# Chains of small numbers on GpSimd, other PSUM tiles and a later sum in a four-layer graph network

## The chip, the cores and the metric

The kernel runs on one core of a Trainium2 chip. The metric is the device time of one execution in microseconds (us). The engines are called as in the profile: PE (TensorE's matmuls), PEld (its weight loads), DVE (VectorE), ACT (ScalarE), POOL (GpSimd), SP (SyncE, which here only issues DMAs).

## What is computed

Four graph layers follow one another on x (4096 nodes x 64 numbers), all with the same dense 0/1 adjacency matrix `adj` (4096 x 4096, 64 MB), each as `x = layernorm(x + layer(x, adj))`:

```python
# layer 0: mean over the neighbours, a linear map, relu, unit length
h = (adj @ x + x) / (adj.sum(1, keepdims=True) + 1)
z = relu(concat([x, h], 1) @ W + b);  y = z / norm(z)
# layers 1 and 3: attention in hyperbolic space
adj_att = sigmoid(left[:, None] + right[None, :] + b_att) * adj
support = einsum('ij,ijd->id', adj_att, logmap(x[:, None], x[None]))
y = proj(expmap(x, support))
# layer 2: the last 100 neighbours, weight halved with each further one
rank = cumsum(adj != 0, axis=1)
y = w(rank) @ (x @ weight) + bias
```

`left` and `right` are one number per node, and `logmap` for a pair of nodes comes down to a function of a bilinear form of the two, so that a 128 x 1024 tile of pairs is a matmul and a few elementwise operations.

## The kernel before

Rows are cut into four groups of 1024 (`GROUPS`, 3 down to 0), columns into 32 blocks of 128 (`BLOCKS`, 31 down to 0). `load` (L655, on SP's queue) brings two blocks of one group, 1 MB, into one of six buffers. Every layer reads the whole matrix once.

**Attention, `attend`.** For one group, a loop over 16 pairs of blocks. For each block of a pair (k = 1, then 0): six matmuls into a tile `z` of 128 x 1024 (two banks of PSUM) from the edges (L945), `hi_lo` (L948) and `src` (L951); on ACT the sigmoid `sig` (L953) and the square `sq` of z (L956); on DVE `max(z, 0) * sig` into half of `t` (L959). For the pair: `(sq + HIGH**2) * t` on 128 x 2048 (L961, DVE). Then four f32 matmuls (eight records, L965) add `xe` times `t` to the group's sums `acc`. PSUM has two `z` tiles (four banks), two `acc` tiles, and two `aux` tiles for everything done by rows: eight banks.

**Row work.** Everything per node stands in generators: `move` (takes the group's sums through `expmap`, `proj`, the residual and the layernorm), `prepare` (the tables of the next attention), `linear` (a 64 x 64 map), `spread_left`, `end_0`, `end_2`. Numbers per node of a group are tiles of 128 x 8, so that nearly all of `move`, L1015 to L1079, is a chain of DVE operations on 8 elements per partition, with three calls of `rsqrt` (L673 to L679, ten operations each) and one tanh on ACT (L1034). Around it stand copies of the rows from `aux` (L1002, ACT), one product on GpSimd (L1007), two reductions on DVE (L1011, L1013), and at the end a product on GpSimd (L1081), one on DVE (L1082) and a sum on DVE (L1085). Row tiles have one buffer each.

**What sets the order.** `later` puts a generator in one of two queues. `tick(n)` counts places, and at each it resumes the generators whose time has come; the number that a generator yields (`soon`, `near`, `after`) is how many places it waits. In attention there are `rate` ticks behind each of a pair's two L959 and behind its L961. `need(tag)` ticks until a part is done. `held` and `free` keep row work from asking for an `aux` tile while another is in use. What is traced in this way is put in order by the framework's planner: in the attention layers it may place row work ahead of pair work on an engine where it thinks it ready; in layers 0 and 2 the order of PE and ACT is that of the program.

**Layer 2.** `count` makes the running count of neighbours: it adds to a tile `z`, by two matmuls for each 512 rows (L1386), what the block before and this one bring. ACT turns it into weights (Exp, L1395), and `add_up` adds weights times `halves` to the sums (four matmuls of 64 columns, L1401). `wide_pass` runs two groups side by side, `narrow_pass` one, twice. In the wide pass PE gets the count of one group, then the sums of the other, one behind.

The loop of the pairs before:

```python
zp = ps.tile([P, WW], F32, name="z")
...
V.scalar_tensor_tensor(t[:, k], zp, 0.0, sig, ALU.max, ALU.mult)
tick(rate)
...
V.scalar_tensor_tensor(t, sq, HIGH**2, t, ALU.add, ALU.mult)
for k in (1, 0):
    j = 2 * g + k
    for h in range(2):
        nc.tensor.matmul(acc[h * D : (h + 1) * D, :], xe[:, j, :], ...)
tick(rate)
```

Of the kernel before, what the change touches and what calls it, by code (L numbers as in the profile page):

```python
# [10 lines left out]
F32 = mybir.dt.float32  # L11
# [10 lines left out]
D = 64  # L22
# [36 lines left out]
def gnn_stack_kernel(  # L59
# [509 lines left out]
    def stream(fits):  # L569

        with ExitStack() as st:
# [9 lines left out]
            aux = pool("f_aux", 2, space=PSUM)  # L581
# [7 lines left out]
            FIXED = {mybir.EngineType.PE, mybir.EngineType.Activation}  # L589
            queues, place, done, held = ([], []), [0, 0], set(), []  # L590

            def tick(n):
                for _ in range(n):
                    place[1] += 1
                    for queue in queues:
                        while queue and queue[0][1] <= place[1]:
# [5 lines left out]
                            if wait:  # L602
                                break

# [24 lines left out]
            def near():  # L629

                return 3 if place[0] == 0 else 1

# [36 lines left out]
            def rsqrt(a, name):  # L669
# [10 lines left out]
                return r  # L680

# [73 lines left out]
            def curved(c, name, least):  # L755


                c2, sc, rsc, of_y, root, short = (
                    num(keep, name + n, 1)
                    for n in ("_c2", "_sc", "_rsc", "_of_y", "_root", "_short")  # L760
# [3 lines left out]
                V.tensor_mul(root, rsc, c)  # L764
                V.tensor_scalar(of_y, rsc, -((2.0 * UNIT) ** -0.5), None, ALU.mult)
# [3 lines left out]
                return c, c2, sc, rsc, of_y, root, short  # L769
# [21 lines left out]
            def prepare(layer, s, att, b_att, curve, least, good, small):  # L791


                c, c2, sc, rsc, of_y, root, short = curve
# [110 lines left out]

            def spread_left(s):
# [17 lines left out]
            def attend(layer, s, rate, then):  # L924
# [3 lines left out]
                acc = ps.tile([P, W], F32, name="acc")  # L928
                for g in reversed(range(NB // 2)):
# [4 lines left out]
                    sq = sb.tile([P, 2, WW], F32, name="sq")  # L934
                    t = sb.tile([P, 2, WW], F32, name="t")
                    for k in (1, 0):
# [3 lines left out]
                        zp = ps.tile([P, WW], F32, name="z")  # L940
                        for h in range(2):
# [9 lines left out]
                            nc.tensor.matmul(half, src[:, of], dst[:, to], start=False, stop=True)  # L951
                        sig = sb.tile([P, WW], F32, name="sig")
# [9 lines left out]
                    for k in (1, 0):  # L962
                        j = 2 * g + k
                        for h in range(2):
                            nc.tensor.matmul(  # L965
                                acc[h * D : (h + 1) * D, :], xe[:, j, :],
                                t[:, k, h * W : (h + 1) * W],
                                start=j == BLOCKS[0], stop=j == BLOCKS[-1],
                            )
                    tick(rate)  # L970
                sums = row.tile([P, W], F32, name="sums", bufs=2)
# [10 lines left out]
            def move(layer, s, sums, curve):  # L982
# [3 lines left out]
                c, c2, sc, rsc, of_y, root, short = curve  # L986
# [22 lines left out]
                yield near()  # L1009
                yield soon()  # L1010
# [4 lines left out]
                V.scalar_tensor_tensor(k, d, c2, sum_1, ALU.mult, ALU.add)  # L1015
                V.tensor_mul(k, k, rb[:, at])

                kx, t2, xt = nums("kx"), nums("t2"), nums("xt")
                V.tensor_mul(kx, k, x2g)
                V.scalar_tensor_tensor(t2, d, -2.0, kx, ALU.mult, ALU.add)  # L1020
                V.tensor_mul(t2, t2, k)
                V.tensor_add(t2, t2, uu)
                V.tensor_scalar(t2, t2, 1e-30, None, ALU.max)
                V.tensor_sub(xt, d, kx)
                yield soon()
# [3 lines left out]
                V.scalar_tensor_tensor(un, t2, root, rsqrt(t2, "r_t2"), ALU.mult, ALU.mult)  # L1029
                V.tensor_scalar(un, un, fac, short, ALU.mult, ALU.max)  # L1030
                th = nums("th")
                V.reciprocal(r_un, un)
# [50 lines left out]
                yield soon()  # L1083
                yield soon()
                V.tensor_add(x_of(layer + 1)[:, at, :], u, w)  # L1085
                yield after(72)

            def linear(layer, s, weights, finish):

# [420 lines left out]
```

## Time and profile before

| | |
|---|---|
| median of 3 runs | 1141.41 us (1140.45 to 1144.33) |
| the profiled execution's own time | 1140.81 us |
| its span, first to last instruction | 1139.1 us |
| PE, DVE, ACT, POOL busy in the span | 1021.6, 956.0, 821.2, 66.1 us |
| layer 0, up to the first L959 | 0 to 191 us |
| layer 1, to its last L961 | 191 to 532 us |
| layer 2, to layer 3's first L959 | 527 to 777 us |
| layer 3, to its last L961 | 777 to 1110 us |
| last `move` and store | 1110 to 1139 us |

A line of the profile's groups or of its timeline has the source line in the kernel, the engine, the operation, `out<-in` by the program's names, and sizes as partitions x elements. In a timeline the first two numbers are the start and the duration in us; the brackets at the end give idle time of the engine before the instruction and what ended it. Records of neighbouring instructions on an engine can overlap a little, so what an instruction takes from its engine is read from start to start. PE's durations are modelled, so there too the spacing is read.

### The profile page before, as it was taken

The page shows a single profiled execution, that of the slowest core. Times are in us where ns is not written, and L with a number is a line of the kernel's source. Part 1 is how long each engine was busy: PE and PEld are TensorE (multiplying, and loading weights), DVE is VectorE, ACT ScalarE, POOL GpSimd, SP SyncE. Part 2 cuts the span into 40 slices and gives each one's busy share as a digit, 9 for nine tenths or more (in the row PEclk, how much of TensorE's full clock was granted, in tenths as well). Part 3 has the DMA queues.
Part 4 walks back from the last instruction along what each step waited for, and adds up shares of the span by engine and source line. Part 5 has one row for each costly group of instructions (what it writes and reads, how often), then busy time and mean ns, then how long its engine had stood idle before and what let it go on. Part 6 is the DMA issues. An engine that isn't in the chain of part 4 may idle for free.

```text
span 1139.1 us, 13626 instructions
## 1 busy us (share of the span) xinstructions
PE 1021.6 (90%) x4949; PEld 391.2 (34%) x4949; DVE 956.0 (84%) x1882; ACT 821.2 (72%) x894; POOL 66.1 (6%) x97
## 2 busy tenths in 40 slices
PE   6999897899999899998999997798899999998981
PEld 3545544233333333332333232232333333333320
DVE  6687898999999899999653476528999999999996
ACT  0003216899989789787766778888898998987970
POOL 0020120000000000100100020000000001001001
PEclk8999998999999999999999999899999999999995
DMA  8999998545666466564988976676455665665500
GB/s 342 422 391 405 373 415 337 196 166 203 215 206 219 154 209 221 180 204 154 322 305 301 341 263 233 233 257 231 164 206 188 218 222 194 222 221 183 196 0 23
DMA packets 38419, 271.58 MB, mean 238 GB/s; under 512 B 4550, under 2 KB 4550, under 8 KB 5574
## 3 DMA queue, kind: packets, MB, share of 16 engines
q1 hardware_dynamic: 37440, 269.50, 65.8%
q10 hardware_dynamic: 902, 1.12, 0.3%
q8 instruction: 41, 0.67, 0.2%
q14 instruction: 36, 0.29, 0.1%
HBM read 269.55 MB, written 1.05 MB: 238 GB/s over the span
## 4 chain that ended last, share of the span: by engine, by line
DVE 53%; PE 29%; ACT 8%; DMA 6%; POOL 2%; issue 2%; ACTq 0%; SPq 0%; POOLq 0%; DVEq 0%
DVE t L959 21%; DVE t L961 20%; PE z L1386 10%; DMA edges<-in_adj_dram 6%; PE acc L1401 5%; PE acc L1243 4%; PE acc L965 2%; ACT sig L953 2%; ACT sq L956 2%; ACT sq L1395 1%; PE aux L1106 1%; PE aux L852 1%; PE z L945 1%; DVE junk L751 1%; PE z L951 1%
## 5 line engine op out<-in xcount | busy, mean ns | idle before, releaser
L953 ACT ACTIVATE sig<-left_b,right 128x1024 f32<-128x1024 f32 x256 | 293.8, 1149 | 46.5 <-DVE t L959 36.5
L959 DVE SCALAR_TENSOR_TENSOR t<-z,sig 128x1024 f32<-128x1024 f32 x256 | 310.0, 1216 | 5.9 <-ACT sq L956 5.0
L956 ACT ACTIVATE sq<-z,turn 128x1024 f32<-128x1024 f32 x256 | 281.5, 1106 | 22.8 <-PE z L951 20.7
L961 DVE SCALAR_TENSOR_TENSOR t<-sq,t 128x2048 f32<-128x2048 f32 x128 | 292.9, 2288 | 0.7
L965 PE MATMUL acc<-t,xe 128*64 128x512 f32 x1024 | 255.2, 611 | 28.5 <-DVE t L961 24.4
L945 PE MATMUL z<-edges,two_i 128*128 128x512 bf16 x512 | 201.7, 394 | 21.5 <-DVE t L959 21.5
L951 PE MATMUL z<-dst,src 74*128 74x512 f16 x512 | 195.2, 381 | 0.0
L948 PE MATMUL z<-lo_hi,hi_lo 128*128 128x512 f16 x512 | 194.1, 379 | 0.0
L1395 ACT ACTIVATE sq<-z,at_edge 128x512 bf16<-128x512 f32 (+1 forms) x192 | 153.0, 830 | 53.3 <-PE z L1386 51.9
L965 PEld LDWEIGHTS acc<-t,xe 128*64 128x64 f32 x1024 | 63.6, 137 | 163.0 <-DVE t L961 85.9
L751 DVE SCALAR_TENSOR_TENSOR t<-edges 128x2048 bf16<-128x2048 f32 x32 | 74.0, 2312 | 44.2 <-DMA edges<-in_adj_dram 44.1
L1386 PE MATMUL z<-edges,pass_by 128*128 128x512 bf16 x248 | 89.6, 401 | 15.9 <-ACT sq L1395 15.8
L945 PEld LDWEIGHTS <-two_i 128*128 128x128 bf16 x512 | 50.2, 98 | 143.8 <-issue 96.6
L1243 PE MATMUL acc<-edges,first 128*128 128x512 bf16 x256 | 80.6, 396 | 20.0 <-DMA edges<-in_adj_dram 19.8
L1386 PE MATMUL z<-edges,enter 128*128 128x512 bf16 x256 | 90.8, 397 | 0.0
L1401 PE MATMUL acc<-sq,halves 128*64 128x512 bf16 x512 | 82.6, 401 | 3.6 <-ACT sq L1395 2.9
L1243 PE MATMUL acc<-edges,third 128*65 128x512 bf16 x256 | 80.5, 396 | 0.0
L751 DVE SCALAR_TENSOR_TENSOR junk<-edges 128x2048 bf16<-128x2048 f32 x32 | 73.1, 2285 | 4.7 <-DMA edges<-in_adj_dram 4.5
L948 PEld LDWEIGHTS <-hi_lo 128*128 128x128 f16 x512 | 50.3, 98 | 68.8 <-issue 25.5
L951 PEld LDWEIGHTS <-src 74*128 74x128 f16 x512 | 49.2, 96 | 67.5 <-issue 2.3
L1081 POOL TENSOR_TENSOR w_att<-x,p 128x512 f32<-128x512 f32 x8 | 12.9, 1615 | 495.0 <-DVE q L1079 495.0
L1243 PEld LDWEIGHTS <-first 128*128 128x128 bf16 x256 | 24.1, 98 | 48.9 <-issue 21.3
(262 smaller groups left out, 771.3 us busy)
## 6 DMA issues: line engine op xcount, KB each, us to landing
edges<-in_adj_dram SPq DMA_DIRECT2D x256, 1024.0 KB, 4.9
x<-in_x_dram SPq DMA_DIRECT2D x4, 256.0 KB
out_dram<-x ACTq DMA_DIRECT2D x4, 256.0 KB
w_sb<-in_L_gnn_W_dram ACTq DMA_DIRECT2D x1, 32.0 KB, 5.1
given<-in_L_gnn_b_dram ACTq DMA_DIRECT2D x1, 0.2 KB
given<-in_L_gnn_bias_dram ACTq DMA_DIRECT2D x1, 0.2 KB
given<-in_L_gnn_b_att_dram ACTq DMA_DIRECT2D x1, 0.0 KB
given<-in_L_gnn_att_b_dram ACTq DMA_DIRECT2D x1, 0.0 KB
```

The source lines that it names most:

```text
L751: V.scalar_tensor_tensor(junk, a, 0.0, a, ALU.not_equal, ALU.not_equal, accum_out=odd[:, n : n + 1])
L945: nc.tensor.matmul(half, two_i, edge[:, at : at + W], start=True, stop=False)
L948: nc.tensor.matmul(half, hi_lo[:, of], lo_hi[:, to], start=False, stop=False)
L951: nc.tensor.matmul(half, src[:, of], dst[:, to], start=False, stop=True)
L953: nc.scalar.activation(sig, left_b, AF.Sigmoid, bias=right[:, j : j + 1])
L956: nc.scalar.activation(sq[:, k], zp, AF.Square, bias=turn, scale=-1.0 / UNIT)
L959: V.scalar_tensor_tensor(t[:, k], zp, 0.0, sig, ALU.max, ALU.mult)
L961: V.scalar_tensor_tensor(t, sq, HIGH**2, t, ALU.add, ALU.mult)
L965: nc.tensor.matmul(acc[h * D : (h + 1) * D, :], xe[:, j, :], t[:, k, h * W : (h + 1) * W], start=j == BLOCKS[0], stop=j == BLOCKS[-1],)
L1243: nc.tensor.matmul(accs[h][:m], lhs[:, j, :], edge[:, at : at + W], start=j == BLOCKS[0], stop=j == BLOCKS[-1],)
L1386: nc.tensor.matmul(z[:, h : h + W], lhs, rhs[:, h : h + W], start=j == BLOCKS[0], stop=True, skip_group_check=True,)
L1395: nc.scalar.activation(w, z[:, :n], AF.Exp, bias=at_edge, scale=-LN2)
```

## The change

- **GpSimd.** In `move`, for every group but a layer's last, the small operations and the last two large ones (L1082, L1085) go from DVE to GpSimd (`class Small`). There a `scalar_tensor_tensor` is two operations. The first step of each `rsqrt` (integers), the reciprocal of `den` and the two reductions stay on DVE. The reciprocal of `un` is replaced by a product and a minimum. The generator's waits become `pool_done(...)`.
- **Order.** `mark` makes every row instruction on PE, ACT or DVE that a tick traces follow, on its engine, the last pair instruction traced before it; from the second group of an attention layer on.
- **PSUM.** Three `z` tiles (six banks), one `acc`, one `aux`. In `end_0` the two halves take the one `aux` tile in turn. Layer 2's wide pass keeps the sums of both groups in the third `z` tile.
- **Sums later.** In `attend` a pair's four matmuls into `acc` come two pairs later, behind the first block's z matmuls of that pair (`in_order`). `sig` has three buffers.
- **Layer 2.** In the wide pass PE gets the counts of both groups, then the sums of both for the block before.
- **`linear` and the stores** behind a group go to the second queue, 9 ticks on, for every group but the last.

```diff
-            aux = pool("f_aux", 2, space=PSUM)
+            aux = pool("f_aux", 1, space=PSUM)
...
+            ROW_ENGINES = FIXED | {mybir.EngineType.DVE}
...
+            def mark(rows):
+                traced = nc.cur_bb.bb.instructions
+                for i in traced[seen[0] :]:
+                    if i.engine not in ROW_ENGINES:
+                        continue
+                    if not rows:
+                        pairs_last[i.engine] = i
+                    elif anchored[0] and i.engine in pairs_last:
+                        tc.add_manual_dep(
+                            i, pairs_last[i.engine].name,
...
+                seen[0] = len(traced)
 
             def tick(n):
                 for _ in range(n):
                     place[1] += 1
+                    mark(False)
...
+                    mark(True)
...
+            def pool_done(small, large=0):
+
+                return 2 + int(small * 0.2 + large * 0.9)
...
+            class Small:
...
+                def stt(self, out, in0, scalar, in1, op0, op1):
+                    if not self.on_pool:
+                        V.scalar_tensor_tensor(out, in0, scalar, in1, op0, op1)
+                        return
+                    t = nums("pool_t")
+                    nc.gpsimd.tensor_scalar(t, in0, scalar, None, op0)
+                    nc.gpsimd.tensor_tensor(out, t, in1, op1)
...
+                def rsqrt(self, a, name, small):
+
+                    r, t = nums(name), nums("rs_t")
+                    if self.on_pool:
+                        yield self.wait(small)
+                    V.tensor_scalar(
+                        r.bitcast(I32), a.bitcast(I32), -0.5, float(0x5F3759DF),
+                        ALU.mult, ALU.add,
+                    )
+                    for _ in range(3):
+                        self.mul(t, r, r)
+                        if self.on_pool:
+                            self.mul(t, t, a)
+                            self.ts(t, t, -0.5, 1.5, ALU.mult, ALU.add)
+                            self.mul(r, t, r)
...
@@ attend
+                def add_up(g, t, behind=None):
+
+                    for k in (1, 0):
+                        j = 2 * g + k
+                        for h in range(2):
+                            it = nc.tensor.matmul(
...
+                            if behind is not None:
+                                in_order(it.ins, behind.ins)
...
-                        zp = ps.tile([P, WW], F32, name="z")
+                        zp = z_tile()
...
+                        if k == 1:
+                            if len(lag) == 2:
+                                add_up(*lag.pop(0), last)
+                            sq = sb.tile([P, 2, WW], F32, name="sq")
+                            t = sb.tile([P, 2, WW], F32, name="t")
+                        sig = sb.tile([P, WW], F32, name="sig", bufs=3)
...
+                    lag.append((g, t))
                     tick(rate)
+                for args in lag:
+                    add_up(*args)
@@ move
+                G = Small(s != GROUPS[-1])
+                yield G.wait(0, 1) if G.on_pool else near()
                 V.tensor_reduce(uu, sq, AX.X, ALU.add)
                 yield soon()
                 V.tensor_reduce(d, w, AX.X, ALU.add)
                 yield soon()
+                yield soon()
+                G.stt(k, d, c2, sum_1, ALU.mult, ALU.add)
+                G.mul(k, k, rb[:, at])
...
+                r = yield from G.rsqrt(t2, "r_t2", 10)
...
+                yield pool_done(19) if G.on_pool else after(29)
                 nc.scalar.activation(th, un, AF.Tanh, scale=lam)
...
+                if G.on_pool:
+                    yield G.wait(14)
                 V.reciprocal(den, den)
...
+                n = yield from G.rsqrt(t, "n", 12)
...
+                r = yield from G.rsqrt(w2, "n", 21)
...
+                E = nc.gpsimd if G.on_pool else V
                 nc.gpsimd.tensor_mul(w, xg, over(p))
+                E.tensor_mul(u, u, over(q))
                 yield soon()
                 yield soon()
+                E.tensor_add(x_of(layer + 1)[:, at, :], u, w)
+                yield pool_done(15, 3) if G.on_pool else after(72)
@@ attention
-            ps = pool("p_ps", 2, space=PSUM)
+            ps = pool("p_ps", 1, space=PSUM)
+
+            def z_tile():
+                return ps.tile([P, WW], F32, name="z", bufs=3)
...
+                    anchored[0] = n > 0
...
-                        last = n + 1 == NW
-                        later(in_turn((layer + 1, s + 1), behind(s + 1)), last, 9 * last)
+                        later(in_turn((layer + 1, s + 1), behind(s + 1)), True, 9)
                     later(move_s)
@@ wide_pass
-                zs = [ps.tile([P, WW], F32, name="z") for _ in two]
+                zs = [z_tile() for _ in two]
+
+                both = z_tile()
+                accs = [both[:, :W], both[:, W:]]
...
                             count(zs[i], behind[i], here, j, WW)
                             behind[i] = here
-                            while lag:
-                                lag.pop(0)()
-                            w = weights_of(zs[i], WW)
...
+                            weights_of(zs[i], WW, w[:, i])
+                            if i == 1:
+                                for of, acc in enumerate(accs if lag else ()):
+                                    add_up(acc, *lag[of])
+                                lag = [(j, w[:, n, :W], w[:, n, W:]) for n in range(2)]
```

## The prediction

> **What bounds the kernel now.** I read the page's slices and chain first, then sums by stage, then timelines of a quiet stretch and of a group change.
>
> ```profile
> DVE  6687898999999899999653476528999999999996
> DVE 53%; PE 29%; ACT 8%; DMA 6%; POOL 2%; issue 2%; ACTq 0%; SPq 0%; POOLq 0%; DVEq 0%
> ```
>
> DVE is full in the two attention layers (slices 8 to 18, 28 to 38), and the chain that ended last runs on it there; layer 2 between them is PE's. The sums by stage, cut where a group of 16 pairs of blocks ends (columns: window, us, then PE, PEld, DVE, ACT, POOL busy, clock, DMA):
>
> ```profile
> 277.60:358.80 81.20, 77.10 (x337) 26.91 (x336) 79.72 (x118) 72.71 (x72) 1.31 (x1) 1.00 0.61 207
> 358.80:445.10 86.30, 81.21 (x360) 29.94 (x360) 82.05 (x125) 74.31 (x76) 2.23 (x2) 1.00 0.58 195
> 532.30:643.00 110.70, 108.54 (x577) 36.16 (x578) 57.09 (x144) 77.08 (x81) 4.99 (x3) 1.00 0.83 298
> ```
>
> Layer 1's groups last about 87, 81.2, 86.3, 87.2 us, layer 3's 86.9, 81.2, 81.1, 83.5. What a pair costs DVE stands in its timeline:
>
> ```profile
> 396.33 1.22 DVE L959 SCALAR_TENSOR_TENSOR t<-z,sig 128x1024 f32<-128x1024 f32 x1
> 397.46 0.15 DVE L678 SCALAR_TENSOR_TENSOR rs_t<-rs_t,t 128x8 f32<-128x8 f32 x1
> 397.54 1.21 DVE L959 SCALAR_TENSOR_TENSOR t<-z,sig 128x1024 f32<-128x1024 f32 x1
> 398.67 0.15 DVE L679 SCALAR_TENSOR_TENSOR r_t<-rs_t,r_t 128x8 f32<-128x8 f32 x1
> 398.78 2.29 DVE L961 SCALAR_TENSOR_TENSOR t<-sq,t 128x2048 f32<-128x2048 f32 x1
> 400.99 0.22 DVE L1029 SCALAR_TENSOR_TENSOR un<-t,k_root,r_t 128x8 f32<-128x8 f32 x1
> ```
>
> From start to start, the three large operations take 1.13 + 1.13 + 2.21 = 4.47 us. A small one slipped between them adds only 0.08 to 0.11: three make the pair 4.74. In layer 1's first group no small ones run, and the pair still takes 4.74 on average; there it is PE:
>
> ```profile
> 249.18 1.94 PE L965 MATMUL acc<-t,xe 128*64 128x512 f32 x8
> 254.04 1.94 PE L965 MATMUL acc<-t,xe 128*64 128x512 f32 x8 [0.17 <-DVE t L961]
> 255.91 0.40 PE L945 MATMUL z<-edges,two_i 128*128 128x512 bf16 x1
> 258.66 1.08 PE L965 MATMUL acc<-t,xe 128*64 128x512 f32 x4
> ```
>
> 258.66 - 254.04 = 4.62 us when PE waits for nothing (1.87 of sums, 2.75 of z), 4.86 in the pair before, since the sums wait for the pair's own L961. So PE's floor, 4.62, lies above DVE's, 4.47. At a group change DVE stands still behind GpSimd:
>
> ```profile
> 382.22 1.19 POOL L1007 TENSOR_TENSOR w_att<-x,u 128x512 f32<-128x512 f32 x1 [12.49 <-ACT u L1002]
> 383.44 0.69 DVE L1013 TENSOR_REDUCE d<-w_att 128x8 f32<-128x512 f32 x1 [3.48 <-POOL w_att L1007]
> ```
>
> and then a dozen dependent small operations, 0.20 us each, run in a row (385.77 to 388.33) ahead of the pairs. That is why 81 to 87 us stand where 16 x 4.62 = 74 would do.
>
> **What the Trainium skill says.** "SBUF — State Buffer", Who interferes with whom: a VectorE operation with two SBUF inputs and a GpSimd operation that reads SBUF exclude each other for the whole instruction. The trace agrees, both ways:
>
> ```profile
> 462.08 2.28 DVE L961 SCALAR_TENSOR_TENSOR t<-sq,t 128x2048 f32<-128x2048 f32 x1
> 462.23 3.04 POOL L1081 TENSOR_TENSOR w_att<-x,p 128x512 f32<-128x512 f32 x1 [78.82 <-DVE q L1079]
> 464.28 1.53 DVE L1082 TENSOR_TENSOR u<-u,q 128x512 f32<-128x512 f32 x1
> ```
>
> L1081 takes 1.04 us elsewhere; here it sits out L961, then L1082 (0.69 alone) sits out it. L959, with z in PSUM, doesn't exclude: L1081 took 1.04 us beside it at 368.69. "Perfetto Trace Analysis", GPSIMD Engine Instruction: time GpSimd from start to start; I do so below. Its section Identifying the Most-Contended Engine warns that matmul busy time misleads; here 77.1 of 81.2 us is a modelled sum, and I use spacings. "TensorEngine Tiling (Array Packing)", Key Properties: a change of tiling mode drains the array. Layer 2's wide pass agrees (z matmuls use 128 columns, sums 64):
>
> ```profile
> 604.38 0.62 PE L1401 MATMUL acc<-sq,halves 128*64 128x512 bf16 x4
> 604.93 0.62 PE L1386 MATMUL z<-edges,pass_by 128*128 128x512 bf16 x2
> 605.39 0.61 PE L1386 MATMUL z<-edges,enter 128*128 128x512 bf16 x2
> 605.94 0.62 PE L1401 MATMUL acc<-sq,halves 128*64 128x512 bf16 x4
> ```
>
> Four z matmuls spaced 0.225 us would take 0.90; to the first sum it is 1.01, and from sums to z 0.31 where sums among themselves take 0.24. A change there and back costs about 0.09 + 0.07 = 0.16 us.
>
> **The change, part by part.**
>
> *Chains to GpSimd* (groups 2 to 4 of each attention layer; each layer's last `move` stays on DVE). Of a chain's 75 small DVE operations, 71 leave, and L1082 and L1085 (0.69 us, up to 1.5 when excluded). DVE keeps the two reductions (0.68 each, about 1.3 spaced), three first steps of rsqrt and a reciprocal (0.1 each). DVE per group: 16 x 4.47 = 71.5, + 1.3 + 0.4 = 73.2 us. GpSimd gets, by count in the new code, 90 small operations (a scalar_tensor_tensor becomes two) and two more large ones. Small GpSimd work in the trace is 0.22 to 0.28 us a record, 0.13 to 0.20 between independent starts (L816 to L821 at 226.31 to 226.77); no row shows dependent ones. Bounds: 0.26 (the record alone) to 0.6 (L818 at 224.87, shut out by DVE's L805); I take 0.33, the record and the 0.07 that L1081 starts behind L1079. With some 60 dependent and 30 independent, 0.28 on average. L961 shuts GpSimd out for 2.2 of every 4.6 us, so about 9 operations fit a pair: 10 pairs, 46 us. With some 10 us until the reductions are done, four large operations (two pairs, 9) and five handovers to DVE or ACT (1 each), a chain is 70 us: inside a group, without much to spare.
>
> *What that costs DVE.* An operation in flight holds up L961: about 0.1 us in 12 pairs, and the large ones 0.7 in all: 2 us. Where DVE or ACT must take a result (after 10 to 21 small operations, for which the new waits allow 4 to 6 ticks of 1.55 us), 15 operations at that pace take 7.7 us against 6.2: 1 to 1.5 late, with the pairs queued behind. Over the touches I take 3 us (0 to 8). DVE: 73.2 + 2 + 3 = 78.
>
> *Three z tiles, sums two pairs behind, row work ordered behind the pairs.* The wait for L961 goes; PE's floor remains: 16 x 4.62 = 73.9, + two L1000 clusters (0.45 each) and L914 (0.9) = 75.7; with `linear` (two x (0.44 + 1.13) = 3.1, groups 3 and 4 of layer 1) 78.8. The stop at the change goes: the reduction stands behind the pairs traced before it, two ticks later. One PSUM tile for rows: PE's next transposes wait for the reader of the last; after L856's copies 0.25 us is left now, after L1117 on DVE up to 2 us isn't hidden, in four places: 0 to 5 us in all, 2 taken. A single sums tile costs nothing: its next first sum comes two pairs later. `linear`, and layer 3's stores on ACT's queue (0.34 us of issue), go 9 ticks later beside `move`, no longer ahead of it: nobody waits for them before the next layer, so nothing.
>
> The later of PE (75.7, 78.8) and DVE (78), and a little because their stops don't coincide: 79 for groups without `linear`, 81.5 with. Against 81.2, 86.3, 87.2: -2.2, -4.8, -5.7; against 81.2, 81.1, 83.5: -2.2, -2.1, -4.5. First groups, 8 quiet pairs at 4.62 for 4.74: -1 each. Sum -23.5.
>
> *Layer 2, counts side by side.* Per block two changes of mode fewer, one there and one back: 0.16 x 32 = -5.2 us. Cover: each Exp (1.11 us) has 1.9 us until its z is written again. If DMA can't follow (336 to 354 GB/s; layer 0 moves 422), the gain is lost.
>
> *Tail.* The copies of the last rows wait 2.50 us for L1085 of the group before; that is off DVE, but GpSimd may end as late: -1 (-2.5 to +3).
>
> Sum: -23.5 + 2 - 5.2 - 1 = -28 from 1140.8, the profiled execution's own time (span 1139.1); the median, 1141.4, is 0.6 above. 1113 us.
>
> **Rivals.**
> (B) PE's floor is reached; GpSimd's chain never holds anything. Groups of 76 and 79: -5, -7, -8 and -5, -5, -7.5, layer 2 and tail as above: -44, so 1097; if the preparation in the first groups lost its stops too, 6 less. For it: DVE has 2.5 us of slack to PE. Against: the exclusion seen at 462.
> (C) GpSimd becomes the bound. If a dependent small operation takes 0.6 us (0.46 on average), a pair holds 6; 90 take 15 pairs, 69 us, and with the same 24 around them a chain is 93. The next group's copy into `u_1` (one buffer) waits on ACT for the chain's last step, and pairs queue behind it. Six groups of about 91 instead of 83.4 on average: +45, less 9 for the rest: 1177. It decides from about 0.5 us per dependent operation on, where the chain passes 84. Against: records of 0.26.
> (D) The steps are right but stops of DVE, ACT and PE add up rather than cover each other: 4 us more in six groups, 1138: no change.
>
> **Chances.** A 0.55 (1113, from 1104 to 1128), B 0.22, C 0.14, D 0.09. A measurement of this kernel tells about 0.3%, 3.4 us, from no change. Faster 0.79, the same 0.06, slower 0.15. The range leaves out the far end of B and most of C: 1096 to 1143.
>
> **What would show it.** Right: quiet pairs near 4.62 us, no wait of L965 for L961, no 3 us stop before L1013, DVE gaps behind POOL rows below 5 us a group, wide pass near 105 us. Wrong: POOL without a pause through a group, ACT or DVE waiting for POOL rows for over 8 us a group, or a group above 84 us.

## The result, and the profile after

The changed kernel took 1142.4 us (median of 20 runs, 1134.9 to 1148.5) where the kernel before took 1141.7 in the same session: a ratio of 1.0007, with a 95% interval of 0.9990 to 1.0023. That is no change that can be measured, where 1113 us had been forecast. Its runs spread more than those of the kernel before (1138.9 to 1144.9), and the longer ones have the lower mean granted clock: 0.965 at 1134.9 us, 0.949 at 1148.5. Its profiled execution has a span of 1140.6 us (before: 1139.1). In what follows a name with a line number is that of the changed kernel: L1062 and L1064 are what L959 and L961 were, L1019 is L965 (the sums), L1138 is tanh.

First the two lines of the page that were shown of before: DVE's slices, then the chain's shares by engine.

```profile
DVE  6587886999979899898653765419999899899874
PE 49%; DVE 31%; ACT 8%; POOL 5%; issue 4%; DMA 3%; ACTq 0%; SPq 0%; POOLq 0%; DVEq 0%
```

DVE had 53% of the chain that ended last and PE 29%; now they have changed places. That much of the plan came true: the work left DVE, and PE became the bound. Yet the span did not fall. A table by stage, cut at the ends of L1064, shows that the gains are there and that something eats them (us; "start" ends with the first L1064, a group is 16 pairs):

| stage | before | after | difference |
|---|---|---|---|
| start and layer 0 | 196.5 | 204.7 | +8.2 |
| layer 1, groups 1 to 4 | 81.1, 81.2, 86.4, 87.2 | 80.7, 82.8, 81.3, 82.0 | -9.1 |
| to the first L1064 of layer 3 | 249.2 | 245.4 | -3.8 |
| layer 3, groups 1 to 4 | 82.4, 81.2, 81.1, 83.4 | 82.3, 82.5, 82.2, 87.0 | +5.9 |
| tail | 29.4 | 29.7 | +0.3 |

Groups with GpSimd's chains, in the sums by stage (columns: window, us, then PE, PEld, DVE, ACT, POOL busy, granted clock, DMA):

```profile
285.40:368.20 82.80, 79.92 (x338) 27.72 (x336) 74.79 (x55) 70.53 (x71) 38.44 (x94) 0.96 0.57 203
368.20:449.50 81.30, 81.14 (x362) 29.89 (x360) 75.47 (x57) 72.25 (x75) 40.57 (x94) 1.00 0.58 207
941.70:1023.90 82.20, 78.39 (x338) 27.51 (x336) 74.78 (x55) 70.42 (x71) 38.44 (x94) 0.98 0.59 208
1023.90:1110.90 87.00, 77.17 (x314) 26.01 (x312) 74.68 (x57) 63.63 (x64) 36.63 (x94) 0.92 0.34 119
```

DVE's busy time in a group without `linear` fell from 79.7 to 74.8 us, and GpSimd's is 38 of 82: no engine is full in 82.80 except PE by its modelled sum, and the granted clock is below 1 in three of the four. The second line is the exception that helps: with `linear` in it, it has more work, a clock of 1.00, and is shorter than the first. Between row work the pairs do run at PE's floor: 4.61 us on average, in turns of 3.46 and 5.76.

What the other groups have and the second hasn't is seen at one place, here in layer 3's second group (the timeline, lines of four engines in order of time):

```profile
881.01 2.22 POOL L741 TENSOR_TENSOR rs_t<-r_t 128x8 f32<-128x8 f32 x1 [4.72 <-DVE r_t L736]
886.71 2.37 POOL L1134 TENSOR_SCALAR r_un<-r_t,k_by_root 128x8 f32<-128x8 f32 x1
889.19 0.33 POOL L1132 TENSOR_SCALAR un<-un,k_short 128x8 f32<-128x8 f32 x1
889.55 0.21 ACT L1138 ACTIVATE th<-un 128x8 f32<-128x8 f32 x1 [4.81 <-POOL un L1132]
892.86 1.23 DVE L1062 SCALAR_TENSOR_TENSOR t<-z,sig 128x1024 f32<-128x1024 f32 x1 [3.92 <-ACT sq L1059]
894.14 0.39 PE L1041 MATMUL z<-edges,two_i 128*128 128x512 bf16 x1 [2.80 <-DVE t L1062]
896.47 3.61 PE L1019 MATMUL acc<-t,xe 128*64 128x512 f32 x8 [0.85 <-DVE t L1064]
900.20 1.23 DVE L1062 SCALAR_TENSOR_TENSOR t<-z,sig 128x1024 f32<-128x1024 f32 x1 [1.52 <-PE acc L1019]
```

Read it downwards. GpSimd stood 4.72 us for the first step of the inverse root, which DVE does (L736) and which stands behind a pair there; it is then shut out by L1064 for 2.22 us instead of 0.20, and once more, 2.37 us, at L1134, which the planner put ahead of `un`. `un` is ready at 889.5. ACT had come to tanh at 884.7 and stands 4.81 us; it makes `sig` and `sq` for the pairs, so DVE stands 3.92 and PE 2.80. Then the eight sums that take 1.94 us elsewhere take 3.61, and DVE waits again, for PE. The reason is PE's clock, the third figure from the end of this line (the sums by stage of the changed kernel, 896.5 to 899.9):

```profile
896.50:899.90 3.40, 3.40 (x8) 0.73 (x8) 2.18 (x2) 3.40 (x4) 0.00 (x0) 0.50 0.00 0
```

A granted clock of 0.50, for 3.4 us. The whole stop costs its group about 5 us (the first experiment shows this). It is there in layer 1's second group and in layer 3's second, third and fourth; in layer 1's third and fourth ACT waits 0.2 us at tanh.

The second stop is in layer 3's last group, on ACT:

```profile
1097.31 0.34 ACTq L1527 DMA_DIRECT2D out_dram<-x  x1
1097.78 1.11 ACT L1059 ACTIVATE sq<-z,turn 128x1024 f32<-128x1024 f32 x1 [6.50 <-POOL x L1193]
```

The store of the group before waits on ACT's queue for GpSimd's last step, and the last four blocks' `sq` wait behind it. `anchored` is off by the time the store is traced, so the planner was free to put it there.

The third is where layer 1 begins:

```profile
192.62 0.18 DVE L1311 RECIPROCAL deg<-aux 128x4 f32<-128x4 f32 x1 [5.85 <-PE aux L1308]
193.29 0.42 DVE L1315 TENSOR_TENSOR z<-z,xw 128x256 f32<-128x256 f32 x1
193.87 1.28 ACT L1056 ACT_TABLE_LOAD   x1 [3.78 <-DVE z L1315]
```

The second half of layer 0's last rows waits its turn for the one PSUM tile, 5.85 us behind the first half; ACT's first sigmoid waits for its last reader of `xw`. From layer 0's last matmul to the first large product it is 18.7 us, where it was 11.8.

### The profile page after: what moved, and what is told of

The parts are those of the page before. It is cut to its first block, busy times and chain, and to the rows that moved or that the text cites. A ratio compares the mean times of both kernels' runs of the same rounds, so it can differ in the third digit from the quotient of the medians.

```text
span 1140.6 us, 13998 instructions
## 1 busy us (share of the span) xinstructions
PE 1030.1 (90%) x4949; PEld 402.2 (35%) x4949; DVE 908.9 (80%) x1450; ACT 803.7 (70%) x896; POOL 285.7 (25%) x649
## 4 chain that ended last, share of the span: by engine, by line
PE 49%; DVE 31%; ACT 8%; POOL 5%; issue 4%; DMA 3%; ACTq 0%; SPq 0%; POOLq 0%; DVEq 0%
PE acc L1019 12%; DVE t L1062 10%; DVE t L1064 9%; PE z L1495 9%; PE z L1041 5%; PE z L1047 4%; PE z L1044 4%; PE acc L1350 4%; PE z L1507 3%; DMA edges<-in_adj_dram 3%; DVE junk L820 2%; ACT sig L1056 2%; PE acc L1507 2%; ACT sq L1502 2%; ACT sq L1059 2%
## 5 line engine op out<-in xcount | busy, mean ns | idle before, releaser
L1062 DVE SCALAR_TENSOR_TENSOR t<-z,sig 128x1024 f32<-128x1024 f32 x256 | 306.9, 1217 | 45.8 <-ACT sq L1059 25.5
L1064 DVE SCALAR_TENSOR_TENSOR t<-sq,t 128x2048 f32<-128x2048 f32 x128 | 295.5, 2309 | 1.6
L1056 ACT ACTIVATE sig<-left_b,right 128x1024 f32<-128x1024 f32 x256 | 288.3, 1145 | 2.7 <-DVE t L1062 2.2
L1019 PE MATMUL acc<-t,xe 128*64 128x512 f32 x1024 | 270.3, 630 | 13.1 <-DVE t L1064 13.0
L1502 ACT ACTIVATE sq<-z,at_edge 128x512 bf16<-128x512 f32 (+1 forms) x192 | 150.7, 829 | 48.4 <-PE z L1495 45.4
L1019 PEld LDWEIGHTS acc<-t,xe 128*64 128x64 f32 x1024 | 65.9, 140 | 148.7 <-issue 84.0
L1350 PE MATMUL acc<-edges,first 128*128 128x512 bf16 x256 | 81.1, 398 | 13.2 <-DMA edges<-in_adj_dram 13.1
L820 DVE SCALAR_TENSOR_TENSOR junk<-edges 128x2048 bf16<-128x2048 f32 x32 | 73.2, 2286 | 6.3 <-DMA edges<-in_adj_dram 6.0
L1105 POOL TENSOR_TENSOR w_att<-x,u 128x512 f32<-128x512 f32 x8 | 10.5, 1317 | 227.4 <-ACT u L1100 227.4
L851 POOL TENSOR_TENSOR sq<-z 128x512 f32<-128x512 f32 x8 | 12.1, 1518 | 195.8 <-DVE z L850 173.1
L1208 ACT COPY x_t<-aux 64x512 f32<-64x512 f32 x16 | 9.2, 572 | 50.5 <-PE aux L1203 50.5
```

What stands on the lines that cost most here:

```text
L820: V.scalar_tensor_tensor(junk, a, 0.0, a, ALU.not_equal, ALU.not_equal, accum_out=odd[:, n : n + 1])
L1019: it = nc.tensor.matmul(acc[h * D : (h + 1) * D, :], xe[:, j, :], t[:, k, h * W : (h + 1) * W], start=j == BLOCKS[0], stop=j == BLOCKS[-1],)
L1056: nc.scalar.activation(sig, left_b, AF.Sigmoid, bias=right[:, j : j + 1])
L1350: nc.tensor.matmul(accs[h][:m], lhs[:, j, :], edge[:, at : at + W], start=j == BLOCKS[0], stop=j == BLOCKS[-1],)
L1502: nc.scalar.activation(w, z[:, :n], AF.Exp, bias=at_edge, scale=-LN2)
```

## The experiments

The theory after these traces (T): the gain came as forecast and was given back at three places where an engine of the pairs meets row work in its own queue: tanh, the store, the start of layer 1. Rivals: (R1) GpSimd's chain is itself too long, so a later reader only moves the wait; (R2) the PSUM tiles and the lag cost as much as they bring; (R3) GpSimd's part isn't what gains. Each ratio below is to the kernel before on the same chip; that of the changed kernel is 1.0007. Differences in us between two runs can be between chips, on which the kernel before took 1141.7 to 1143.0 us. The diffs show only the lines that matter.

**Tanh one pair later.**

```diff
-                yield pool_done(19) if G.on_pool else after(29)
+                yield pool_done(19) + 3 if G.on_pool else after(29)
```

> The step of ACT that takes tanh of GpSimd's `un` is traced 3 ticks later: it stands 15 blocks into a group instead of 13, one pair of 4.6 us later; nothing else is changed. Theory T (ACT reaches tanh before GpSimd has `un`, and the pairs stop behind it): the four stops of 4.8 us vanish, with the half-clock stretches of PE that follow them; groups L1 g2 and L3 g2, g3 lose 2 to 4 us each, L1 g3 and g4 (no stop there) stay at 81.3 and 82.0; 7 to 12 us off, a ratio of 0.990 to 0.994 to the changed kernel. Rival R1 (GpSimd's chain is itself too long for a group): the stop moves to another reader of the chain (the next group's copies, or the store), groups stay within 1 us, total 1140 to 1145.

Measured: 1118.3 us, 0.9781 (0.9750 to 0.9813): 24 us less, by one number. ACT waits for GpSimd's `un` in no group any more. Layer 1's second group fell from 82.8 to 77.7, layer 3's from 82.5, 82.2, 87.0 to 77.7, 77.4, 78.6; layer 1's third and fourth, where there had been no stop, stayed (81.7, 81.0). T's mechanism holds; its size was put too low, since each stop gave back the whole 5 us and the last group more. In that group ACT still waits 6.11 us for the store, in front of the last two blocks, so its 8.4 us and the 4.8 us of the next run overlap: both mends together give 11.4. R1 falls: from its first large product to its last sum a chain takes 66 to 74 us in the kernels with the later tanh, in groups of 76 to 82, so its length is not the limit.

**The store behind the last pair.**

```diff
-                anchored[0] = False
+                anchored[0] = layer == 3
```

> The rows of layer 3 stay ordered behind the pairs to the end of the layer, so the store of the group before last stands on ACT's queue behind the last pair (block 32) instead of ahead of its last four blocks (28); nothing else is changed. Theory T (the store waits on ACT for GpSimd's last step, and the pairs wait behind it): the last group falls from 87 to about 82, the tail stays near 30 us: 4 to 6 us off, a ratio near 0.995 to the changed kernel. Rival R1 (the chain's end is what the tail waits for): the stop moves into the tail, no change.

Measured: 1134.5 us, 0.9923 (0.9900 to 0.9947). The last group fell from 87.0 to 82.2 and the tail from 29.7 to 27.7: 6.8 of the 7.9 us between the medians, as T expected and a little more. (Layer 0's end varies between 178 and 185 us from one profiled execution to the next, so a stage's us count for more than a span's.)

**The halves of layer 0's last rows in z tiles.**

```diff
+                        wide = place[0] == 1
+                        if wide:
+                            t = z_tile()[:, : SB * P].rearrange("p (k f) -> p k f", k=SB)
+                        else:
+                            yield from free()
+                            t = take(F32, P, SB, P)
...
```

> From layer 1 on, the two halves of layer 0's last rows take one z tile each, at once, instead of the one PSUM tile for rows in turn with the transposes; layer 0 itself is left as it is. Theory T (one PSUM tile for rows delays the second half, whose addition of `xw` ACT's first sigmoid waits for): the first large product of layer 1 starts 6 to 8 us sooner, the rest is unchanged: about 7 us off, a ratio near 0.994. Rival (the delay comes from layer 0 before, or from the planner's other order): under 2 us off.

Measured: 1139.4 us, 0.9963 (0.9946 to 0.9980), but not by what was expected: from layer 0's last matmul to the first large product it was 19.3 us, not less than 18.7. The z tiles lie where layer 0's sums lay, so the first half began only when ACT had copied them (188.6, layer 0's last matmul at 182.6), at half clock. The edit moved the wait; it neither shows nor refutes that the turns are the cause.

**Two buffers of `sig`.**

```diff
-                        sig = sb.tile([P, WW], F32, name="sig", bufs=3)
+                        sig = sb.tile([P, WW], F32, name="sig")
```

> `sig` has two buffers again instead of three; nothing else is changed. Theory T (the third buffer lets a third sigmoid of layer 3 be issued in the middle of layer 2's narrow pass, with two loads of ACT's tables around it, 3.7 us, while PE stands and then runs at half clock): the narrow passes fall from 137.5 to about 132.5 us; the quiet pairs stay at 4.6. 3 to 5 us off, a ratio near 0.996. Rival R2 (the third buffer is what lets pairs reach PE's floor): quiet pairs rise to 4.7 to 4.9 us, groups by 1 to 3 us, the total is the same or higher.

This is what had been seen in the changed kernel's narrow pass of layer 2, on ACT:

```profile
710.54 1.28 ACT L1056 ACT_TABLE_LOAD   x1
711.83 1.15 ACT L1056 ACTIVATE sig<-left_b,right 128x1024 f32<-128x1024 f32 x1
713.00 1.28 ACT L1502 ACT_TABLE_LOAD   x1
```

A sigmoid of layer 3 is taken ahead, three times instead of two, each for 3.7 us of ACT with two table loads, while PE waits. Measured: 1143.5 us, 1.0005 (0.9987 to 1.0023): nothing. The third sigmoid left this pass, for the start of layer 3, but the narrow passes fell by only 1.6 us, and layer 1's first group rose from 80.7 to 84.2. T was wrong on this one.

**Three mends together**: the later tanh, the store behind the pairs, and no pause between the halves from layer 1 on.

```diff
-                        if h == 0:
+                        if h == 0 and place[0] == 0:
                             yield near()
```

> Three mends of the changed kernel together: tanh 3 ticks later; layer 3's rows, its stores too, behind the pairs to the end; and from layer 1 on the second half of layer 0's last rows right behind the first, with no pause for other row work between. Theory T: the later tanh alone gave 1118.3; the store behind the last pair takes some 3 to 4 us more off (the last group's stop of 3.8 us at the store goes, the tail falls from 30 to 28), and the two halves together let layer 1 start 4 us sooner: 1108 to 1113. Rival R1 (the chain's own length is the next limit): the last group or the tail gives it back, 1115 to 1119.

Measured: 1114.4 us, 0.9783 (0.9757 to 0.9810). The medians lie 4 us under the later tanh alone; the ratios don't tell the two apart. From layer 0's last matmul to the first large product it is 17.1 us, only 1.7 less. Groups now (sums by stage of this kernel: layer 1's second and third, layer 3's third):

```profile
283.70:361.40 77.70, 76.79 (x332) 27.14 (x336) 75.16 (x56) 70.67 (x71) 38.69 (x94) 1.00 0.59 219
361.40:443.10 81.70, 80.78 (x354) 29.92 (x360) 75.81 (x57) 72.48 (x75) 36.52 (x94) 1.00 0.55 206
943.40:1020.80 77.40, 76.46 (x332) 27.17 (x336) 74.96 (x55) 70.75 (x72) 38.66 (x95) 1.00 0.60 221
```

Set beside the changed kernel's lines: DVE's and GpSimd's busy times are the same, the clock is 1.00, and 82.80 has become 77.70, 82.20 has become 77.40. Where the 28.0 us of span went: tanh in three groups 14.7, the last group 11.4, the start 1.8, all else 0.1.

**The mends with the chain on DVE.**

```diff
-                G = Small(s != GROUPS[-1])
+                G = Small(False)
```

> The same three mends, but the small chains of `move` stay on DVE in every group, in the form and with the pauses of the kernel before; PSUM tiles, lagging sums and the order behind the pairs stay changed. Theory T (GpSimd's part is a gain once its readers don't wait): some 73 small operations a group at 0.08 to 0.11 us between the large ones, 6 to 8 us, and the two products and the sum of 0.69 us come back to DVE, groups of 80 to 83 instead of 77 to 79, and more in the tail: 1130 to 1142. Rival R3 (small operations fit into DVE's slack, PSUM and order make the gain): within 6 us of the three mends.

Measured: 1149.4 us, 1.0067 (1.0049 to 1.0084), 35 us over the three mends. Layer 1's groups are 78.9, 85.2, 80.8 and layer 3's 78.8, 82.2, 79.3, but the chains now run over the ends of their groups: layer 2 took 252.5 and the tail 37.0 us. (Of the 33.6 us between the two spans, 3.4 lie before layer 0's last matmul, which the edit doesn't touch.) R3 falls: with this order of rows GpSimd's part is a gain, more than T had said. That the loss comes from chains which end too late is read from layer 2 and the tail; a DVE chain with places of its own was not tried.

**The kernel before with one PSUM tile for rows**, and `end_0` as in the changed kernel.

```diff
-            aux = pool("f_aux", 2, space=PSUM)
+            aux = pool("f_aux", 1, space=PSUM)
...
```

> The kernel before, with one PSUM tile for rows instead of two and the halves of layer 0's rows in turn as in the changed kernel; nothing else. Theory T (this is what delays the start of layer 1): from layer 0's last matmul to the first large product 18 to 19 us instead of 11.8, everything else within 3 us: 5 to 9 us slower than before, a ratio of 1.005 to 1.008. Rival (the delay belongs to the ordering of rows or to the z tiles): 12 to 13 us there, ratio 0.999 to 1.002.

Measured: 1158.8 us, 1.0162 (1.0142 to 1.0183). From layer 0's last matmul to the first large product it was 17.2 us instead of 11.8, so the turns do delay layer 1, by 5.4; and elsewhere it cost more than expected: 8 us in layer 1's first group, where the preparation of the next groups takes the tile too, and 5 in the tail. In the changed kernel that first group is 80.7; that the lag covers such waits of PE there is likely, but not shown.

**The later tanh without the lag**: two z tiles, two sums tiles, two for rows, sums behind their own pair.

```diff
-                return ps.tile([P, WW], F32, name="z", bufs=3)
+                return ps.tile([P, WW], F32, name="z", bufs=2)
...
-                            if len(lag) == 2:
-                                add_up(*lag.pop(0), last)
...
-                    lag.append((g, t))
+                    add_up(g, t)
...
```

> The changed kernel with the later tanh, but PSUM as in the kernel before: two z tiles, two sums tiles, two for rows, each pair's sums right behind it, and layer 2's two sums in their own tiles with its counts still side by side. GpSimd's chains and the order behind the pairs stay. Theory T (both parts are needed: DVE's floor falls by GpSimd, PE's waits by the lag): quiet pairs of 4.74 to 4.9 instead of 4.62, groups of 80 to 82 instead of 77.5 to 79 (81.5 with `linear`): 1130 to 1140, 12 to 20 us over the later tanh alone. Rival R2 (the lag and the third z tile bring nothing, since DVE was the bound and GpSimd freed it): within 4 us of 1118.

Measured: 1162.3 us, 1.0171 (1.0147 to 1.0195), 44 us over the later tanh alone. Quiet pairs are 4.59 and 4.88 in turn, as T said, but the groups are 85 to 92: each cluster of row work stops the pairs for 2 to 4.6 us, where the lag and the third tile had kept PE fed. R2 falls, and by more than T's number: with the order behind the pairs the lag and the third tile are needed. The run doesn't part the two from each other.

**Layer 0's `xw` and weights in memory of their own**, with the three mends.

```diff
-                xw = own.tile([P, NB, D], F32, name="xw")
+                xw = keep.tile([P, NB, D], F32, name="xw")
...
```

> The three mends, and layer 0's `xw`, `sum_w` and `count_w` stay in memory of their own, so that nothing of the attention layers' work tiles lies where they lay (`top` and `low` still do). Theory T' (layer 1's first sigmoid waits for the last reader of `xw`, since its tile lies in that memory): ACT's table load comes 5 to 8 us sooner, the first large product 3 to 6 us sooner, about 4 us off the three mends: 1108 to 1112. Rival (the whole work memory of layer 0 is waited for together, or DVE's own order decides): under 1.5 us off.

Measured: 1112.6 us, 0.9730 (0.9693 to 0.9768), the best of all, though not apart from the three mends by its interval. ACT's table load now comes before the last L1315, and the first large product 15.3 us after layer 0's last matmul instead of 17.1: 1.8 us, between the theory's 3 and its rival's 1.5. Of the 6.9 us lost at the start, 3.5 are still there.

**Layer 2's wide order alone, in the kernel before**: its `wide_pass` is the changed kernel's, but for the sums' tiles.

```diff
-                both = z_tile()
-                accs = [both[:, :W], both[:, W:]]
+                accs = [ps.tile([P, W], F32, name="acc") for _ in two]
...
```

> The kernel before with layer 2's wide pass in the new order alone: both groups' counts, then both groups' sums, two sums tiles as before. Theory T (the two changes of tiling mode less per block are worth 0.16 to 0.22 us, whatever else is changed): the wide pass falls by 5 to 7 us, the rest within 2 us, a ratio of 0.994 to 0.996. Rival (the wide pass got shorter by what ended before it): within 2 us, 0.998 to 1.002.

Measured: 1138.7 us, 0.9958 (0.9943 to 0.9974). From the first count to the first of the next pass it took 103.7 us instead of 111.8, and the narrow passes behind it 3.7 more. At their first row work PE now stands 4.1 us instead of 2.5, and 6.8 us of half clock go with it instead of 3.4. Net 4.3 us in layer 2.

**Tanh two ticks sooner, and two pairs later**, each with the other two mends.

```diff
-                yield pool_done(19) + 3 if G.on_pool else after(29)
+                yield pool_done(19) - 2 if G.on_pool else after(29)
...
+                yield pool_done(19) + 6 if G.on_pool else after(29)
```

> The three mends, but tanh 2 ticks sooner than the changed kernel has it (12 blocks into a group, where it had 13 and the mends 15). Theory T (what counts is where ACT meets GpSimd's chain): a stop of 4 to 7 us in all six groups, those without one in the changed kernel too, PE at half clock after each: 30 to 45 us over the three mends, 1144 to 1160. Rival (the later tanh only happened on a better plan of the instructions): no order by place, within 10 us of the mends.

> The three mends, but tanh 6 ticks later than in the changed kernel, two pairs instead of one (17 blocks into the first such group, later in each that follows, since the chain then runs over a group's end). Theory T (one pair was enough to clear the stop; beyond it nothing is won, and the last chain ends later): groups stay at 77 to 82, the tail grows by 3 to 8 us: 1115 to 1125. Rival (each tick later is a gain, the stops are not gone yet): below 1112.

Sooner: 1125.3 us, 0.9845 (0.9809 to 0.9882). A stop in all six groups, as expected, but of 4.4 us in four and 1.6 in two, and a stop of 4.4 us cost its group only 1.9 to 2.2, in one case 3.6. That case is the only one of the six with half clock behind it. So this expectation failed on size: 11 us, not 30 to 45. In layer 3's second group:

```profile
881.02 0.27 POOL L1134 TENSOR_SCALAR r_un<-r_t,k_by_root 128x8 f32<-128x8 f32 x1
881.76 0.21 ACT L1138 ACTIVATE th<-un 128x8 f32<-128x8 f32 x1 [4.47 <-POOL un L1132]
884.28 0.39 PE L1041 MATMUL z<-edges,two_i 128*128 128x512 bf16 x1 [1.82 <-DVE t L1062]
886.48 1.94 PE L1019 MATMUL acc<-t,xe 128*64 128x512 f32 x8 [0.72 <-DVE t L1064]
```

The stop came before that pair's L1064, so L1134 was not shut out (0.27 us instead of 2.37) and `un` came sooner too; PE stood in two parts, and the sums ran at full clock. In all ACT stands at tanh for as long as in the changed kernel (20.9 us against 19.5), yet the groups lie only 9.2 us above those of the three mends, where three groups of the changed kernel alone lose 14.7. So the place counts, but not as "the later, the better": a stop costs what PE stands, and half clock on top where it follows.

Two pairs later: 1115.5 us, 0.9744 (0.9707 to 0.9781). No stop, the chains run over the ends of groups, the tail 32.3 us. One pair is enough, more brings nothing.

**`r_un` behind tanh**, to see what its place ahead of `un` costs.

```diff
-                G.ts(r_un, r, by_root, 1.0 / fac, ALU.mult, ALU.mult)
-                G.ts(r_un, r_un, by_short, None, ALU.min)
...
                 nc.scalar.activation(th, un, AF.Tanh, scale=lam)
+                G.ts(r_un, r, by_root, 1.0 / fac, ALU.mult, ALU.mult)
+                G.ts(r_un, r_un, by_short, None, ALU.min)
```

> The changed kernel with the two operations of `r_un` traced behind tanh instead of ahead of it; tanh stays 13 blocks into a group. Theory (1): GpSimd takes `un` at once, some 2.4 us sooner, ACT's stop falls from 4.8 to about 2.4 us, PE stands less than 2 us and keeps its clock; L1 g2 and L3 g2, g3 fall from 82.5 to 78 to 79.5: 12 to 18 us under the changed kernel, 1124 to 1131. Rival (the order on GpSimd is not what is late; DVE's first step of rsqrt is): stops within 1 us of 4.8, the total within 4 us of 1142.

Measured: 1142.9 us, 1.0003 (0.9982 to 1.0023). The edit didn't reach the queue: the planner still put `r_un` ahead of `un` on GpSimd (from 888.36 us on, for 2.37, in layer 3's second group), and all stops are as they were. What `r_un`'s place costs was thus not tried.

**Stops of ACT of known length**, with the three mends, in quiet pairs without row work.

```diff
+                        stops = {(1, 2): 2, (1, 1): 3, (1, 0): 4, (3, 2): 5, (3, 1): 6, (3, 0): 8}
+                        more = stops.get((layer, s), 0) if (g, k) == (6, 1) else 0
+                        for _ in range(1 + more):
...
```

> The three mends, and in one quiet pair of each of the six groups behind a layer's first ACT does the same sigmoid 2, 3, 4 (layer 1), 5, 6, 8 (layer 3) times more, 1.04 us each; the values are the same. It stops the pairs for known times. Theory (2): PE stands about N x 1.04 less 1 to 2 us; up to a stop of PE of some 2 us (N = 2, 3) the clock stays full and the group loses no more than PE stood; from some 2.5 us on (N = 4 or 5 and above) 3.4 us of half clock follow and the group loses 1 to 1.7 us more. In all 18 to 26 us over the three mends. Rival (the half clock belongs to the row work and its fp32 transposes, or comes at random): no half clock behind any of the six stops, or behind short ones as well.

Measured: 1139.7 us, 0.9974 (0.9958 to 0.9991), 25 us over the three mends. Five and six sigmoids more (the timeline of PE in this kernel, lines with a wait, and the sums behind them):

```profile
908.79 0.39 PE L1041 MATMUL z<-edges,two_i 128*128 128x512 bf16 x1 [1.64 <-DVE t L1065]
912.13 1.94 PE L1019 MATMUL acc<-t,xe 128*64 128x512 f32 x8 [0.53 <-DVE t L1067]
...
991.50 0.58 PE L1041 MATMUL z<-edges,two_i 128*128 128x512 bf16 x1 [3.67 <-DVE t L1065]
994.83 2.69 PE L1019 MATMUL acc<-t,xe 128*64 128x512 f32 x8 [0.19 <-DVE t L1067]
```

PE stood 1.64 us and kept its clock; it stood 3.67 and the sums behind took 2.69 instead of 1.94, in 6.8 us of half clock. Eight more: 7.78 us and 10.2 of half clock. Two to four more: PE stood 0.8 us at most, no half clock. The groups against those of the three mends: -1.2, +2.0, -0.3, +3.3, +6.4, +12.2 for 2.1, 3.1, 4.2, 5.2, 6.2, 8.3 us of ACT. The theory holds in kind: half clock follows the stop itself, without row work, and not the short stops. It set in at six more, not at four or five, because PE stood less than expected at those. At eight the group lost 3.9 us more than ACT's extra work.

## Why the prediction was wrong, step by step

- **PE's floor of 4.62 us a pair**: right. 4.61 in quiet stretches.
- **Chains on GpSimd**: right in size. A dependent small operation has a pitch of 0.28 us (0.33 taken), an independent one 0.16, one shut out 2.1 to 2.5; a chain is 64 to 68 us (70 taken). DVE's busy time is 74.8 us a group (73.2 forecast, and 2 for being held up).
- **"Five handovers to DVE or ACT (1 each)", and "over the touches I take 3 us (0 to 8)"**: here it failed. A handover isn't 1 us: DVE's first step of the inverse root stands in its queue behind a pair, so GpSimd gets it 4.7 us later, and two operations that are shut out on the way add some 4. "1 to 1.5 late" was worked out from the pace of 15 small operations alone; `un` came 4.8 late in four of six groups. And the reader is ACT, which feeds every pair: PE stood 2.7 to 3.7 us and ran at half clock for 3.4 or 6.8, which the sum didn't have at all. Runs: one pair later, 24 us less. The prediction's own signs of being wrong fit only in the last group (87.0 us, over 84, with 4.81 and 6.50 us of ACT's waits, over 8); elsewhere they were set too wide to show a stop of 4.8.
- **The store: "nobody waits for them before the next layer, so nothing"**: failed. ACT waited for it 6.5 us, in front of the last pairs; 4.8 us in the last group and 2.0 in the tail. An issue of 0.34 us has the price of what it waits for.
- **One PSUM tile for rows: "0 to 5 us in all, 2 taken"**: too low. Only the places behind L1117 were looked at. The one that cost, 6.9 us, is the start of layer 1; 5.4 of them come from the turns alone, by the run in the kernel before.
- **The stop at the change of groups, the wait for L961**: right for the stop: none of 3 us is left before L1112. The wait fell from 24.4 us in all to 13.0, most of it at the begin and end of a layer or behind the stops.
- **79 us a group, 81.5 with `linear`**: with the three mends 77.7, 77.7, 77.4, 75.6 and 81.7, 81.9, against 82.8, 82.5, 82.2, 87.0 and 81.3, 82.0 in the changed kernel. First groups gained 0.4 and 0.1 us, not 1. The forecast's sum, -28 us, is nearly what the mended kernel has, 1114.4 against 1113, but partly by luck: by stages its attention groups gained 28.8 us (23.5 forecast), the start lost 6.4 (2 taken), layer 2 and the tail gained 4.0 (6.2).
- **Layer 2's order, -5.2**: right in sum (-4.3 to -4.8 alone), made of -8.1 in the wide pass and +3.7 given back behind it, which had not been seen. In the changed kernel the narrow passes took 5.7 us more; 3.7 are of that kind, 1.6 went with the third sigmoid, the rest stays open. (The forecast's own figures, 1.01 us against 0.90, give 0.11 for the change there, not 0.09.)
- **Tail, -1**: +0.3, and -1.7 with the store moved.

Rival D ("stops add up", 1138) had the nearest number, but not its cause: it spread 4 us over six groups, while the stops are few, each at a reader in a queue, and go away with that reader's place. C, GpSimd as the bound, fell, and so did its point of decision: it came to 0.28 us, far from 0.5. (Its sum was also too mild: at 0.46 us each, the 2.4 us that L961 leaves free hold 5 operations, not 6.) B's groups of 76 were nearly reached by the mended kernel.

## What to carry to other kernels

When a chain of small operations is moved to a slower, shared engine, price not its length but its handovers: for each, find the queue in which the reader stands, what is behind it there, and how late the producer can be when every step of it may sit out one long operation. Put the reader a full period later than the sum says; a place too late was free here over one to two pairs, a place 4.8 us too early cost most of the gain. Count a stop of PE not by its length alone but by the slow clock that may follow. Then search the same queues for instructions that the change has merely moved, DMA issues among them.

## What the runs showed of the hardware

PE's clock follows its stops. Over the sixteen profiled executions of this study, leaving out the wait at each one's start, there are 99 stops of PE of 2.5 us or more; at 91 of them half clock set in between 1 us before their begin and 3.5 us after their end. Of 339 stops of 0.8 to 1.5 us this holds for only 85. The stretches last 3.41 us or a multiple. The Trainium skill, "TensorE: Matmul & The Clock Gate", section HAM oscillation — how this bites in real kernels, gives "no PE-idle gaps >~3.4µs" as its rule, and Part 1 of the page a free-running window of 3413 ns. The length of the stretches agrees; the threshold here is lower, since stops of 2.5 to 3 us were followed by half clock in 42 of 46 cases.

How a stop lies in that window tells more than its length. Within each trace all begins and ends of half clock lie on one grid of 3.413 us, 403 of them to within 0.02 us. Of the intervals of this grid at full clock, all 116 in which PE's (modelled) records fill less than 40% were followed by half clock, 76 of 155 with 40 to 60%, and 14 of 4571 with more. The four alike stops of the run with tanh sooner, 1.7 to 1.8 and 0.7 us of PE each, left 0.61, 0.58, 0.43 and 0.53 in their emptiest interval, and only the third brought half clock. So a stop of 4.4 us on ACT that leaves PE standing 2.5 us in two parts can cost 2 us or 3.6, and one of 4.8 costs 5.

Where an operation of GpSimd is shut out can be told from its record: in the changed kernel 0.20 to 0.30 us became 2.12 to 2.45, near L1064's own 2.31, seven or eight times in each chain of 94.
